# A recurrence with experts behind it: another order for the end of a half, the next preparation, the experts and the skip gate

## The chip, the cores and the metric

The kernel runs on one core of a Trainium2 chip. The metric is device time in microseconds (us) for one execution; the time of a version is the median over its runs. A core has five engines with a queue each: PE (matmul; its weight loads are listed as PEld), DVE (vector), ACT (scalar), POOL (GpSimd) and SP, which here only issues transfers. Each engine takes its instructions in the order of its queue; between engines they wait on semaphores. PE's clock can be granted at less than full speed, and the profile shows the granted share.

## The reference, cut to what matters

Eight layers run one after the other on x of 4 x 1024 tokens with 128 features. The change touches the last two: a selective recurrence with 16 states over 256 channels, and a mixture of eight experts. Each layer adds its result to x and is followed by a layer norm.

```python
# recurrence
x = resid * rsqrt(mean(resid * resid) + EPS) * norm_w
skip = x @ skip_w.T                        # 256 channels
xs = silu(conv4(x @ in_w.T) + conv_b)
delta = softplus(xs @ wd1.T @ wd2.T + wd2_b)
Bm, Cm = xs @ wb.T, xs @ wc.T              # 16 states each
def step(h, inp):                          # along the tokens
    d_l, b_l, c_l, x_l = inp
    h = exp(d_l[:, :, None] * A) * h + (d_l * x_l)[:, :, None] * b_l[:, None, :]
    return (h, einsum('ben,bn->be', h, c_l))
y = (ys + xs * W_D) * silu(skip)
return resid + y @ out_w.T
# experts, all eight computed, gated per token
probs = softmax(x @ Wr + br)
keep = mask of the largest probs up to TOP_P = 0.8
h = relu(einsum('bth,ehf->betf', x, W1) + b1)
y = einsum('betf,efh->beth', h, W2) + b2
return einsum('bte,beth->bth', probs * keep, y)
```

## The kernel before

The last two layers are worked in eight halves: four sequences, two halves of 512 tokens each (`b`, `h`). All is float32. For each half there are four stages, each written as a generator that yields between its steps, so that one loop, `l3`, can interleave them:

- `l3_prepare`: norm and transpose (`sq3`, `xnT`), two products `pxe` with a four-tap convolution on DVE and a silu by tanh (`xs`), the product `pdb`, whose rows for B and C go to memory (`rows`), and then delta: the products `pd0`, `pd1`, a softplus on ACT and DVE (`sp_u`, `sp_w`, through an exponential and a logarithm), and `ud` = delta times `xs` on DVE and `dl` on ACT. It takes ten steps.
- `l3_scan`: sixteen states, one step each. SP loads the state's rows of B and C, broadcast over the partitions (`bn`, `cn`). POOL multiplies `db` = `ud` x `bn` (L1845). ACT makes `da` (L1849), DVE runs the scan along the tokens (L1850, two of them for the 256 channels), POOL multiplies `hc` = `db` x `cn` (L1861). `db` and `hc` have four buffers each. The first half of a sequence hands its last column on as `carry`.
- the states are summed in PSUM by identity products, `pys` (`add`). From the third half on (`b > 0`), `hc` of each odd state is first added to the even one before it by an adding transfer (L1865), and the sum is taken up two states later. `l3_sum` takes up what is left after the last state and adds `xs` times `W_D`.
- `l3_finish`: the skip gate (`psk`, tanh, two DVE operations for each half of the channels), the output product `po`, the residual `ss_r`, the norm, and the router of the experts, which ends in `gt`. The half then goes to the list `todo` with `age` 0.

The experts (`l3_experts`, `l3_ffn_head`, `l3_ffn`) take halves from `todo` once they are older than three states. A head (`pgt`, `gT`, `pb2`) starts the accumulator `h_acc`. Each of the eight experts has four products `ph` with relu on ACT (`hh`), sixteen products `py`, and four operations of DVE into `h_acc` (L1989). Weights (`wh`) are loaded two experts ahead.

In the loop of `l3`, each state of the running half is followed by one step of the end of the half before it (`l3_sum`, then `l3_finish`), one step of the preparation of the next half, one of what is left of the layer before (a mixture with sorted rows: `moe`, its gathers `yg` on POOL and its tiles `wx` on PE), and three or four steps of the experts. What is left of the end and of the preparation after the sixteenth state is written out then.

This order of the text isn't yet the order of the queues: the framework schedules the instructions for each engine when the program is built, and the queue is fixed from then on.

Of the kernel before, what the change touches and what calls it, by code (L numbers as in the profile page):

```python
# [10 lines left out]
F32 = mybir.dt.float32  # L11
I32 = mybir.dt.int32
U32 = mybir.dt.uint32
AF = mybir.ActivationFunctionType
ALU = mybir.AluOpType
# [3 lines left out]
P = 128  # L19
# [21 lines left out]
E3, NST, DDELTA, KCONV = 256, 16, 64, 4  # L41
# [17 lines left out]
class Net:  # L59
# [1535 lines left out]
    def l3(self, moe, fp):  # L1595

        c3 = self.c3  # L1600
        halves = [dict(b=b, h=h) for b in range(B) for h in range(2)]
        for i, u in enumerate(halves):
            u["prev"] = halves[i - 1] if u["h"] else None
        halves[0] = dict(self.c3["first"], **{k: halves[0][k] for k in ("prev",)})
        for i, u in enumerate(halves[1:], 1):
            u["prev"] = halves[i - 1] if u["h"] else None
        work = self.l3_experts(fp)
        end = iter(())
        for i, u in enumerate(halves):
            nxt = iter(())  # L1610
            if i + 1 < len(halves):
                if halves[i + 1]["h"] == 0:
                    while "done" not in self.m2["st"][halves[i + 1]["b"]]:
                        next(moe)
                nxt = self.l3_prepare(halves[i + 1])
            for f in self.l3_scan(u):
                next(end, None)
                next(nxt, None)
                for k in range(1):
                    next(self.m2["rest"], None)  # L1620
                busy = next(moe, moe) is not moe
                if i == 0:
                    for k in range(1):
                        next(moe, None)
                for k in range(3 if busy else 4):
                    next(work)
                for v in c3["todo"]:
                    v["age"] += 1
            for f in chain(end, nxt):
                pass  # L1630
            end = chain(self.l3_sum(u), self.l3_finish(u))
        for f in end:
            next(work)
        c3["all"] = True
        for f in work:
            pass

    def l3_experts(self, fp):


        c3 = self.c3
        heads, self.wh = [], {}

        def others():

            while len(heads) < 2 and c3["todo"] and ("all" in c3 or c3["todo"][0]["age"] > 3):
                heads.append((c3["todo"].pop(0), []))
            return heads[1:]

        i = 0  # L1650
        while True:
            others()
            if "all" in c3 and c3["banks"]:

                c3["banks"].close()
                c3["banks"] = None
                c3["ctx"].enter_context(self.banks(ff=8))
            if heads:
                u = heads[0]
                if not u[1]:  # L1660
                    yield from self.l3_ffn_head(*u, fp)
                yield from self.l3_ffn(*u, i, fp, others)
                heads.pop(0)
                i += NE
            elif "all" in c3:
                return
            else:
                yield
# [146 lines left out]
    def l3_scan(self, u):  # L1815


        nc, c3, b, h = self.nc, self.c3, u["b"], u["h"]
        sp, wp, aneg = c3["sp"], c3["wp"], c3["aneg"]
        wout = c3["we"][:, :, ND:]  # L1820
        xnT, xs, dl, ud, rows = (u[k] for k in ("xnT", "xs", "dl", "ud", "rows"))
        carry = wp.tile([P, 2, NST], F32, name="carry") if h == 0 else u["prev"]["carry"]
        u["carry"] = carry
        u["py"] = py = []
        u["sums"] = sums = []

        def add(n, hc):
            if not py:
                py.extend(self.psb(f"y{ec}", [P, 512], f"pys{ec}") for ec in range(2))
                u["first"] = n  # L1830
            for ec in range(2):
                self.mm(py[ec], self.ident, hc[:, ec, :], n == u["first"], n == NST - 1)

        u["add"] = add
        for n in range(NST):
            bc = []
            for i, nm in enumerate(("bn", "cn")):
                t = wp.tile([P, 1, 512], F32, name=nm, bufs=4)
                r = i * NST + n
                nc.sync.dma_start(  # L1840
                    out=t[:, 0, :], in_=rows[r : r + 1, :].to_broadcast([P, 512])
                )
                bc.append(t.to_broadcast([P, 2, 512]))
            db = wp.tile([P, 2, 512], F32, name="db", bufs=4)
            nc.gpsimd.tensor_mul(db, ud, bc[0])  # L1845
            for ec in range(2):
                j = ec * NST + n
                da = self.psb("da", [P, 512], "da")
                nc.scalar.activation(da, dl[:, ec, :], AF.Exp, scale=aneg[:, j : j + 1])  # L1849
                nc.vector.tensor_tensor_scan(  # L1850
                    db[:, ec, :],
                    da,
                    db[:, ec, :],
                    carry[:, ec, n : n + 1] if h else 0.0,
                    ALU.mult,
                    ALU.add,
                )
            if h == 0:
                nc.scalar.copy(carry[:, :, n : n + 1], db[:, :, 511:512])
            hc = wp.tile([P, 2, 512], F32, name="hc", bufs=4)  # L1860
            nc.gpsimd.tensor_mul(hc, db, bc[1])  # L1861
            if n % 2 and b > 0:

                hc0 = sums.pop()[1]
                nc.gpsimd.dma_start(out=hc0, in_=hc, accum_op=ALU.add)  # L1865
                sums.append((n, hc0, n + 2))
            else:
                sums.append((n, hc, n + 2))
            for k in range(2):
                if sums and sums[0][2] <= n:  # L1870
                    add(*sums.pop(0)[0:2])
            yield

    def l3_sum(self, u):

        while u["sums"]:
            u["add"](*u["sums"].pop(0)[0:2])
            if u["sums"]:
                yield
        for ec in range(2):  # L1880
            x = u["xs"][:, ec, :]
            self.nc.vector.scalar_tensor_tensor(
                x, x, self.col("W_D", i=ec), u["py"][ec], ALU.mult, ALU.add
            )

    def l3_finish(self, u):


        nc, c3, b, h = self.nc, self.c3, u["b"], u["h"]
        sp, wp = c3["sp"], c3["wp"]  # L1890
        ff = lambda s, n: self.psb("ff", s, n)
        wout = c3["we"][:, :, ND:]
        yt = u["xs"]
        for ec in range(2):
            p = ff([P, 512], "psk")
            self.mm(p, c3["wskip"][:, 0, ec * P : (ec + 1) * P], u["xnT"])

            t = sp.tile([P, 512], F32, name="th")
            nc.scalar.activation(t, p, AF.Tanh, scale=0.5)
            nc.vector.scalar_tensor_tensor(p, t, 1.0, p, ALU.add, ALU.mult)  # L1900
            nc.vector.scalar_tensor_tensor(
                yt[:, ec, :], yt[:, ec, :], 0.5, p, ALU.mult, ALU.mult
            )
            yield
        po = ff([P, 4, D], "po")
        for k in range(4):
            for ec in range(2):
                self.mm(
                    po[:, k, :],
                    yt[:, ec, k * P : (k + 1) * P],  # L1910
                    wout[:, ec, :],
                    ec == 0,
                    ec == 1,
                )

        r = sp.tile([P, 4, D], F32, name="ss_r", tag="s2")
        nc.vector.scalar_tensor_tensor(
            r, self.xN[b][:, 4 * h : 4 * h + 4, :], 2.0, po, ALU.mult, ALU.add
        )
        yield  # L1920
        yield from self.norm_parts(wp, r, b, 4 * h, 4, ps=ff, act=True, slow=True)
        yield
        n = NC // 2
        pr, g, rank, pj, cum = self.router(sp, b, c3["wr"], c3["br"], ps=ff, c0=4 * h, n=n)
        q, cum = cum
        nc.vector.tensor_mul(g, q, pj)
        nc.vector.reduce_sum(cum, g, AX.X)

        nc.vector.tensor_single_scalar(cum, cum, TOP_P, ALU.is_lt)
        nc.vector.scalar_tensor_tensor(cum, rank, 1.0, cum, ALU.is_le, ALU.max)  # L1930
        u["gt"] = sp.tile([P, n, NE], F32, name="gt", bufs=8)
        nc.vector.tensor_mul(u["gt"], pr, cum)
        u["age"] = 0
        c3["todo"].append(u)
# [268 lines left out]
```

## Time and profile before

The median of 23 runs is 2343.95 us, from 2334.18 to 2350.4.

| what | value |
|---|---|
| profiled execution | 2342.13 us, of which span 2340.4 us |
| granted clock of PE, mean | 0.92 |
| PE busy | 2007.0 us, 86% |
| DVE busy | 1349.4 us, 58% |
| ACT busy | 1204.8 us, 51% |
| POOL busy | 1024.3 us, 44% |
| `hc` on POOL (L1861) | 128 of 2483 ns |
| `db` on POOL (L1845) | 128; the form of 112 takes 2606 ns |
| scans on DVE (L1850) | 256, of 1207 and 1267 ns |
| `pys` on PE | 320 records, busy 160.5 us |
| adding transfers `hc<-hc` | 48, 512 KB each, 6.6 us to landing |

The profile names an instruction by its line, its engine and the tiles that it writes and reads. A float32 matmul leaves two records. Busy time of PE is a union of overlapping records, since matmuls are pipelined, so that the mean of one times their number is more than the busy time. The layers before the recurrence fill about the first 1400 us of the span; a second stretch, to about 2200 us, holds the eight halves, and the rest the experts of the last two halves. A row of a timeline gives start, length, engine, line, operation, tiles and, in brackets, how long the engine was idle before it and what ended that. A row of windows gives the stretch, its length, then busy time and instruction count of PE, PEld, DVE, ACT and POOL, PE's granted clock, the share of DMA and its GB/s.

### The profile page before, as it was taken

The page shows a single profiled execution, that of the slowest core. Times are in us where ns is not written, and L with a number is a line of the kernel's source. Part 1 is how long each engine was busy: PE and PEld are TensorE (multiplying, and loading weights), DVE is VectorE, ACT ScalarE, POOL GpSimd, SP SyncE. Part 2 cuts the span into 40 slices and gives each one's busy share as a digit, 9 for nine tenths or more (in the row PEclk, how much of TensorE's full clock was granted, in tenths as well). Part 3 has the DMA queues.
Part 4 walks back from the last instruction along what each step waited for, and adds up shares of the span by engine and source line. Part 5 has one row for each costly group of instructions (what it writes and reads, how often), then busy time and mean ns, then how long its engine had stood idle before and what let it go on. Part 6 is the DMA issues. An engine that isn't in the chain of part 4 may idle for free. (4 is left out here: it accounts for less than half of the span.)

```text
span 2340.4 us, 46470 instructions
## 1 busy us (share of the span) xinstructions
PE 2007.0 (86%) x17858; PEld 1408.3 (60%) x17858; DVE 1349.4 (58%) x3661; ACT 1204.8 (51%) x2619; POOL 1024.3 (44%) x813
## 2 busy tenths in 40 slices
PE   6667978979999999999989856778899989799988
PEld 3455654544577777787777654345565556456666
DVE  6458743433445554654555536877777777676421
ACT  6543433332244444454455536566767876657343
POOL 5100220000123244134143239988898988779400
PEclk9657989979999999999999868989999999899899
DMA  3000110013000010031232056556776676666421
GB/s 104 0 17 21 32 36 10 10 65 115 1 3 3 2 37 22 25 87 37 74 87 74 22 171 178 175 164 196 196 204 176 173 196 164 177 177 180 99 59 50
DMA packets 138702, 211.63 MB, mean 90 GB/s; under 512 B 18613, under 2 KB 75952, under 8 KB 138096
## 3 DMA queue, kind: packets, MB, share of 16 engines
q1 hardware_dynamic: 126192, 173.87, 24.6%
q0 software_dynamic: 12288, 34.79, 7.0%
q8 instruction: 141, 2.31, 0.4%
q14 instruction: 81, 0.66, 0.1%
HBM read 160.29 MB, written 23.16 MB: 78 GB/s over the span
## 5 line engine op out<-in xcount | busy, mean ns | idle before, releaser
L1061 POOL TENSOR_TENSOR qt<-r_q,sb_c_turn 128x256 f32<-128x256 f32 (+1 forms) x256 | 163.8, 661 | 453.2 <-ACT r_q L1053 447.6
L1861 POOL TENSOR_TENSOR hc<-db,cn 128x1024 f32<-128x1024 f32 x128 | 314.8, 2483 | 60.0 <-PE pys L127 25.5
L1845 POOL TENSOR_TENSOR db<-ud,bn 128x1024 f32<-128x1024 f32 x112 | 285.9, 2606 | 32.1 <-DVE ud L1809 15.8
L127 PEld LDWEIGHTS py<-wh,hh 128*128 128x128 f32 x2048 | 250.8, 195 | 70.6 <-issue 35.9
L127 PE MATMUL ph<-xT,wh 128*128 128x512 f32 x512 | 261.6, 628 | 24.3 <-ACT hh L1973 9.9
L127 PE MATMUL py<-wh,hh 128*128 128x128 f32 x2048 | 257.2, 280 | 15.9 <-ACT hh L1973 13.8
L1973 ACT ACTIVATE hh<-ph,sb_cols 128x512 f32<-128x512 f32 x256 | 171.4, 681 | 135.2 <-PE ph L127 108.3
L1119 DVE TENSOR_TENSOR a<-pa_m,sb_c_near 128x256 f32<-128x256 f32 x256 | 96.7, 420 | 213.7 <-PE pa_m L127 213.7
L1076 ACT ACTIVATE kN<-kp_mo,sb_c_trig 128x128 f32<-128x128 f32 x448 | 129.7, 371 | 132.4 <-PE kp_mo L131 119.6
L1849 ACT ACTIVATE da<-dl,aneg 128x512 f32<-128x512 f32 x224 | 153.4, 689 | 75.0 <-DVE db L1850 74.1
L127 PE MATMUL pys<-hc,sb_c_ident 128*128 128x512 f32 x320 | 160.5, 627 | 16.0 <-POOL hc L1861 9.2
L1850 DVE TENSOR_TENSOR_SCAN db<-da,carry,db 128x512 f32<-128x512 f32 x128 | 157.2, 1267 | 10.8 <-ACT da L1849 6.2
L127 PEld LDWEIGHTS ph<-xT,wh 128*128 128x128 f32 x512 | 91.3, 199 | 114.5 <-issue 56.0
L1850 DVE TENSOR_TENSOR_SCAN db<-da,db 128x512 f32<-128x512 f32 x128 | 149.8, 1207 | 11.5 <-ACT da L1849 5.7
L1989 DVE SCALAR_TENSOR_TENSOR h_acc<-py,gt,h_acc 128x128 f32<-128x128 f32 x256 | 71.7, 343 | 134.6 <-PE py L127 134.5
L127 PE MATMUL pqk<-xT,wE 128*128 128x256 f32 x512 | 139.2, 396 | 8.0 <-ACT coT L1195 4.3
L127 PEld LDWEIGHTS pys<-hc,sb_c_ident 128*128 128x128 f32 x320 | 60.8, 203 | 78.4 <-issue 57.4
L127 PEld LDWEIGHTS pqk<-xT,wE 128*128 128x128 f32 x512 | 90.7, 198 | 22.3 <-DVE cv L1038 8.1
L1195 ACT COPY coT<-pt 128x512 f32<-128x512 f32 x64 | 37.5, 585 | 127.1 <-PE pt L131 127.1
L729 POOL DMA_INDIRECT orows<-o,ix x20 | 18.9, 944 | 185.8 <-DVE o L727 160.3
L131 PE MATMUL pt<-sb_c_ident,xN 128*128 128x128 f32 x224 | 54.2, 341 | 51.9 <-ACT xN L174 33.4
L127 PE MATMUL po<-ht,wD 128*128 128x512 f32 x192 | 94.1, 598 | 0.0
(450 smaller groups left out, 4370.1 us busy)
## 6 DMA issues: line engine op xcount, KB each, us to landing
wx<-in_wF SPq DMA_DIRECT2D x92, 384.0 KB, 3.3
bn<-rows SPq DMA_DIRECT2D x128, 256.0 KB, 5.1
cn<-rows SPq DMA_DIRECT2D x128, 256.0 KB, 4.5
wh<-in_wH SPq DMA_DIRECT2D x64, 512.0 KB, 3.6
hc<-hc POOLq DMA_DIRECT2D x48, 512.0 KB, 6.6
xrows<-zero SPq DMA_DIRECT2D x4, 1472.0 KB, 9.0
xg<-xrows SPq DMA_DIRECT2D x20, 256.0 KB, 2.9
yrows<-ys SPq DMA_DIRECT2D x20, 256.0 KB, 3.1
```

The lines of the kernel that those rows point to most:

```text
L127: return self.nc.tensor.matmul(out=out, lhsT=lhsT, rhs=rhs, start=start, stop=stop)
L131: self.nc.tensor.transpose(out, in_, self.ident[0:n, 0:n])
L1061: nc.gpsimd.tensor_mul(u["qt"][:, m, a:], u["q"][:, a:], c2["turn"][:, m, o + a : o + 2 * P])
L1076: self.nc.scalar.activation(u["kN"][:, c, m, :], pk[:, c, :], AF.Copy, scale=trig[:, k, m : m + 1])
L1119: nc.vector.tensor_mul(u["a"][:, i, :, :], pa[i], self.c2["near"][:, None, :].to_broadcast([P, 2, P]),)
L1195: nc.scalar.copy(oT, pt)
L1845: nc.gpsimd.tensor_mul(db, ud, bc[0])
L1849: nc.scalar.activation(da, dl[:, ec, :], AF.Exp, scale=aneg[:, j : j + 1])
L1850: nc.vector.tensor_tensor_scan(db[:, ec, :], da, db[:, ec, :], carry[:, ec, n : n + 1] if h else 0.0, ALU.mult, ALU.add,)
L1861: nc.gpsimd.tensor_mul(hc, db, bc[1])
L1973: nc.scalar.activation(ht, ph, AF.Relu, bias=self.col("h_b1", i=e * NK + k))
L1989: nc.vector.scalar_tensor_tensor(acc[:, c, :], py[:, c, :], gt[:, c, e : e + 1], acc[:, c, :], ALU.mult, ALU.add,)
```

## The change

The loop of `l3` takes two steps of the end of the half before per state instead of one. The next half's preparation takes no step in the first four states and one in each of the other twelve. A half is given to the experts from the first state after its router instead of the fourth. The experts get three steps a state in the last half too. The last half's last odd state isn't added by a transfer but summed as it is. The skip gate moves from `l3_finish` to a function of its own, `l3_gate`, which is called in the states 9 and 12 of the half itself and keeps its result in SBUF (`th0`, `th1`, one buffer each) until `l3_sum`; there DVE adds `W_D` times `xs` into the sum in PSUM and multiplies the gate in.

```diff
-            for f in self.l3_scan(u):
-                next(end, None)
-                next(nxt, None)
+            u["final"] = final = i + 1 == len(halves)
+            for n, f in enumerate(self.l3_scan(u)):
+                for k in range(2):
+                    next(end, None)
+                if n > 3:
+                    next(nxt, None)
                 for k in range(1):
                     next(self.m2["rest"], None)
                 busy = next(moe, moe) is not moe
...
-                for k in range(3 if busy else 4):
+                for k in range(3 if busy or final else 4):
                     next(work)
...
-            while len(heads) < 2 and c3["todo"] and ("all" in c3 or c3["todo"][0]["age"] > 3):
+            while len(heads) < 2 and c3["todo"] and ("all" in c3 or c3["todo"][0]["age"] > 0):
                 heads.append((c3["todo"].pop(0), []))
...
             nc.gpsimd.tensor_mul(hc, db, bc[1])
-            if n % 2 and b > 0:
-
+            if n in (9, 12):
+                self.l3_gate(u, n // 12)
+            if n % 2 and b > 0 and not (u["final"] and n == NST - 1):
                 hc0 = sums.pop()[1]
                 nc.gpsimd.dma_start(out=hc0, in_=hc, accum_op=ALU.add)
...
         for ec in range(2):
-            x = u["xs"][:, ec, :]
+            x, p = u["xs"][:, ec, :], u["py"][ec]
             self.nc.vector.scalar_tensor_tensor(
-                x, x, self.col("W_D", i=ec), u["py"][ec], ALU.mult, ALU.add
-            )
+                p, x, self.col("W_D", i=ec), p, ALU.mult, ALU.add
+            )
+            self.nc.vector.scalar_tensor_tensor(
+                x, u["gate"][ec], 0.5, p, ALU.mult, ALU.mult
+            )
+
+    def l3_gate(self, u, ec):
+
+        nc, c3 = self.nc, self.c3
+        p = self.psb("ff", [P, 512], "psk")
+        self.mm(p, c3["wskip"][:, 0, ec * P : (ec + 1) * P], u["xnT"])
+        t = c3["sp"].tile([P, 512], F32, name=f"th{ec}")
+        nc.scalar.activation(t, p, AF.Tanh, scale=0.5)
+        nc.vector.scalar_tensor_tensor(t, t, 1.0, p, ALU.add, ALU.mult)
+        u.setdefault("gate", []).append(t)
...
-        for ec in range(2):
-            p = ff([P, 512], "psk")
-            self.mm(p, c3["wskip"][:, 0, ec * P : (ec + 1) * P], u["xnT"])
-
-            t = sp.tile([P, 512], F32, name="th")
-            nc.scalar.activation(t, p, AF.Tanh, scale=0.5)
-            nc.vector.scalar_tensor_tensor(p, t, 1.0, p, ALU.add, ALU.mult)
-            nc.vector.scalar_tensor_tensor(
-                yt[:, ec, :], yt[:, ec, :], 0.5, p, ALU.mult, ALU.mult
-            )
-            yield
```

## The prediction, before the changed kernel ran

> **What bounds the kernel now.** I read first the busy row of POOL over the span, then the windows cut at the end of each half's last `hc`, then POOL's and PE's timelines at the seam between two halves, then the chain of waits there.
>
> ```profile
> span 2340.4 us, 46470 instructions
> POOL 5100220000123244134143239988898988779400
> 1498.00:1607.00 109.00, 82.23 (x365) 52.98 (x366) 79.01 (x141) 67.81 (x136) 91.93 (x50) 0.89 0.53 160
> 1903.00:1990.00 87.00, 82.80 (x412) 54.54 (x411) 59.92 (x108) 57.35 (x99) 76.05 (x38) 1.00 0.68 177
> 1990.00:2094.00 104.00, 90.63 (x425) 57.70 (x424) 73.97 (x143) 67.98 (x119) 81.60 (x41) 0.92 0.65 175
> 2094.00:2193.00 99.00, 87.74 (x431) 56.96 (x430) 69.45 (x139) 63.65 (x99) 81.23 (x40) 0.93 0.63 173
> 2193.00:2337.00 144.00, 132.10 (x696) 92.69 (x695) 34.24 (x120) 56.03 (x88) 0.88 (x1) 0.94 0.19 54
> ```
>
> POOL is at 8 to 9 tenths from 1400 to 2200 us: that is the recurrence, eight halves of sixteen states (columns of the windows: length, then busy PE, PEld, DVE, ACT, POOL, granted clock). After it PE alone works for 144 us on experts that are left. Half 5 (1903 to 1990) takes 87 us; halves 6 and 7 take 104 and 99 with nearly the same POOL work. The seams say why:
>
> ```profile
> 1982.63 0.87 POOL L1865 DMA_DIRECT2D hc<-hc  x1
> 1988.10 2.34 POOL L1861 TENSOR_TENSOR hc<-db,cn 128x1024 f32<-128x1024 f32 x1 [4.60 <-PE pys L127]
> 2007.42 9.26 POOL L1845 TENSOR_TENSOR db<-ud,bn 128x1024 f32<-128x1024 f32 x4 [15.81 <-DVE ud L1809]
> 2091.55 2.35 POOL L1861 TENSOR_TENSOR hc<-db,cn 128x1024 f32<-128x1024 f32 x1 [5.13 <-PE pys L127]
> 2107.45 9.26 POOL L1845 TENSOR_TENSOR db<-ud,bn 128x1024 f32<-128x1024 f32 x4 [12.37 <-ACT dl L1810]
> ```
>
> POOL stands idle 17.0 us (1990.4 to 2007.4) and 13.5 us (2093.9 to 2107.45) between the last `hc` of a half and the first `db` of the next, which needs `ud`, the end of the preparation. At the earlier seams the next half's `db` starts up to 17 us ahead of the last `hc`, and no seam shows. The chain through the second seam:
>
> ```profile
> 2094.20 7.36 DMA hc<-hc
> 2101.60 1.14 PE pys L127 x2
> 2103.43 0.69 DVE pd L1808
> 2106.03 0.60 DVE ud L1809
> 2106.66 0.58 ACT dl L1810
> ```
>
> The adding transfer lands, PE sums it, DVE passes its wait for that sum, and only then come the last steps of the preparation, queued behind it.
>
> **The change part by part.** The arithmetic keeps its counts: per half two `psk` products, two tanh, six DVE operations, before and after. Removed is one adding transfer of the last half, for which two identity products come (2 x 0.9 us of PE, in a queue that waits there anyway). What changes is order, and this I read from the queues as built for both kernels; they hold no time, so each stretch is counted in matmuls of 512 columns and priced at 0.90 us (four `ph`, x8 in the records, take 3.60).
>
> *Experts earlier.* Behind the last `pys`, PE had 15.75 experts left and has 11.75. Before, from the end of that `pys` (2204.0) to the first `pgt` of the last half (2249.3) went 45.3 us, and from there to the end 91.1 with ten experts. Now nine follow `pgt`: 91.1 - 8.3 = 82.8 (ten took 2249.3 to 2332). To `pgt` goes the chain: two sums and two gate products on DVE 2.9, `po` 1.9, then `ss_r` to `gt` as before (2224.85 to 2241.53, 16.7), and 2 in PE's queue: 23.5. The gate's `psk`, which came 12 us after the last `pys`, no longer stands in it. Tail 106.3 against 136.4: -30.1. From last `hc` to last `pys` went 11.1 with the transfer; without, as at the first seam (1497.9 to 1499.9), 2.0, and I take 2.5: -8.6.
>
> *The preparation later.* It starts four states later, and its `pd` products, which feed the ACT chain to `ud`, move past the half's last `pys`. In PE's queue before, they stood 23 to 62 matmuls ahead of it at five seams and 7 to 9 ahead at the last two. Now they end 19 behind it (seam 1-2), 6.5 (2-3), 17 (4-5), 6.5 (5-6) and 6.5 (6-7); only 0-1 (9 ahead) and 3-4 (23 ahead) stay open. PE takes its queue in order, so at five seams the whole chain now runs after the half's end. Its price:
>
> ```profile
> 2091.30 1.88 PE L127 MATMUL pd<-db,sb_s_d 65*128 65x512 f32 x4
> 2092.36 0.60 ACT L1795 ACTIVATE sp_u<-pd 128x512 f32<-128x512 f32 x1 [1.66 <-PE pd L127]
> 2098.73 1.06 ACT L1802 ACTIVATE sp_w<-sp_w 128x1024 f32<-128x1024 f32 x1
> 2101.60 1.98 PE L127 MATMUL pys<-hc,sb_c_ident 128*128 128x512 f32 x4 [2.69 <-DMA hc<-hc]
> ```
>
> Last `hc` to the end of `pys` takes 13.4, 9.7 and 11.1 at the three ends that have a transfer last, 11.4 in the mean; 2.0 without. Then PE's stretch to `pd`: 6.5 x 0.90 = 5.9, or 15.3 and 17.1. From `pd`'s end (2093.18) to the logarithm's (2099.79) 6.6, at the seam before 7.5: 7.05. Then two sums and two products on DVE, 2.7. Four `hh` of 0.69 now stand inside ACT's chain: 0 to 2.8, I take 1.4. So a seam costs 28.4 (2-3, 5-6, 6-7), 37.8 (4-5) and 30.2 (1-2, no transfer; eight gathers of 1.26 fill 10 of it). At 0-1 it is 3: nine matmuls ahead is 8 us, the chain 11. Behind these waits on DVE stand the experts' `h_acc`; PE has three to four and a half experts (24 to 37 us) queued ahead of the next `pys`, so it has work for most of a seam. SP's loads of the next `bn` and `cn` (5.1 and 4.5 us) wait for `rows`, written before `pd`; they land inside the seam, and without that cover would cost about 6.
>
> *Bodies.* First `db` to last `hc` took 86.5 and 85.5 in halves 6 and 7: 86 with transfers; half 0, 98.8 with sixteen gathers at 1.26, is 78.6 without. Half 1: 3 + 78.6 = 81.6. Half 2: 30.2 + 86 + 10.1 (eight more gathers) = 126.3; PE's queue has 134 matmuls there, at 0.94 us (the 785 of the whole rest were busy 740 us) also 126. Half 3: 28.4 + 86 + 20.2 (sixteen gathers) + 2.3 (one `db` of half 4) = 136.9. Half 4, no seam: 84. Half 5: 123.8. Half 6: 114.4. Half 7: 113.4 with one transfer less. Sum 780.4 against 695.0 (1497.9 to 2192.9): +85.4.
>
> **Sum:** +85.4 - 8.6 - 30.1 = +46.7 on the profiled run's 2342.1 (its span 2340.4 and 1.7 around it): 2388.8. The median of the runs is 1.8 above that run: 2390.
>
> Granted clock: half 5 without a seam had 1.00, halves 6 and 7 with one 0.92 and 0.93. [...]
>
> **Rivals.**
> (1) The seams stay as they were and the experts' gain is paid out: -8.6 - 30.1 gives 2305. For it: the end's two steps a state free `xs` and the shared tiles earlier, and before, five of seven seams cost nothing. Against: `pd` stands behind the last `pys`. It decides if POOL's added idle stays under 39 us, under half of what I count.
> (2) PE is the true bound and the seams only move its idle about. For it: PE is busy 82.8 of 87 us in half 5, and experts now lie ready to fill a seam. PE's rest after the first half is 792 matmuls against 785, with 100 us of idle unchanged: +7, 2351. Against: halves 6 and 7 show 13 and 11 us of PE idle with experts queued.
> (3) The crowded halves 2 and 3 (134 and 122 matmuls) bind PE and POOL by turns, PE's in-order waits for `hc` holding experts back: half 2 runs at the 92% of half 3 (104.3 of 113), half 3 too loses 8, and ACT's `hh` cost their full 2.8: +26, 2416.
>
> **How the numbers follow.** My forecast 0.66, with its own range 2361 to 2424 (low: transfer 9.7, no `hh`, bodies 2 shorter; high: 13.4, 2.8, bodies 2 longer, half 2 at 92%). Rival 1 0.10, rival 2 0.12, rival 3 0.12, mostly inside that range. The range goes down to 2346 to take in rival 2. A measurement here tells about 0.2% (4.7 us) from no change: faster 0.10, within 0.05 (the low part of rival 2), slower 0.85.
>
> **What would show it.** Right: in POOL's timeline five idle stretches of 25 to 40 us ended by `ud` or `dl` ahead of four `db` in a row (10 us of gathers inside the first); `pd` after the last `pys` at these seams; last `pys` near 2286 and some 106 us behind it. Wrong: the seams under 15 us each, or `pd` on PE before the last `pys`; a tail still of 130 us; or half 2 and 3 stretched with POOL waiting for `pys` instead of `ud`.

## The result, and the profile after

The changed kernel takes 2414.91 us (median of 8 runs, 2404.71 to 2418.93) against 2342.78 us of the kernel before beside it (62 runs): ratio 1.0305, 95% interval 1.0288 to 1.0321, so slower by 72 us. Lines of the page of its profiled execution, with the row of `db` on POOL:

```profile
span 2411.9 us, 46476 instructions
PE 2033.9 (84%) x17862; PEld 1419.6 (59%) x17862; DVE 1358.0 (56%) x3661; ACT 1204.6 (50%) x2617; POOL 1022.4 (42%) x812
...
POOL 5001310000232252242243188948488939494900
...
L1848 POOL TENSOR_TENSOR db<-ud,bn 128x1024 f32<-128x1024 f32 x112 | 284.1, 2650 | 130.5 <-DVE ud L1812 71.8
```

The same row of the kernel before:

```profile
L1845 POOL TENSOR_TENSOR db<-ud,bn 128x1024 f32<-128x1024 f32 x112 | 285.9, 2606 | 32.1 <-DVE ud L1809 15.8
```

POOL's row over the span, at 7 to 9 through the recurrence before, now falls to 3 or 4 in five slices, one at each seam that opens. `db` waits 130.5 us in all where it waited 32.1. The windows cut at the last `hc` of a half (length, busy PE, PEld, DVE, ACT, POOL, granted clock) come next: the seven halves behind the first, then the tail (from the last `hc` of all to the end), then half 2:

```profile
1501.00:2295.00 794.00, 670.97 (x3145) 434.34 (x3146) 527.78 (x996) 492.00 (x895) 591.07 (x303) 0.92 0.59 161
2295.00:2411.90 116.90, 98.21 (x530) 69.15 (x528) 27.66 (x101) 41.88 (x68) 0.04 (x1) 0.93 0.16 49
1577.50:1723.70 146.20, 124.90 (x659) 87.40 (x659) 94.90 (x203) 98.01 (x203) 95.77 (x55) 0.95 0.65 179
```

The first two of these windows in the kernel before:

```profile
1497.90:2192.90 695.00, 606.89 (x2935) 395.20 (x2936) 510.83 (x971) 476.35 (x870) 592.26 (x303) 0.95 0.65 180
2192.90:2340.40 147.50, 132.20 (x697) 92.78 (x695) 34.24 (x120) 56.03 (x88) 0.91 (x2) 0.93 0.19 54
```

The recurrence is 99 us longer, the tail 30.6 shorter, half 0 ends 3.1 later: 71.5 in all. POOL's work in it is the same (591 and 592 us). PE is busy 30 us longer over both windows together (769.2 against 739.1), with 43 records more in them (3675 against 3632, most of them left over from the layer before), and idle 38 us longer (141.7 against 103.4). POOL's timeline at the seams 1-2, 4-5 and 6-7 (in brackets the idle time before):

```profile
1619.03 9.29 POOL L1848 TENSOR_TENSOR db<-ud,bn 128x1024 f32<-128x1024 f32 x4 [18.62 <-DVE ud L1812]
...
1946.99 2.34 POOL L1864 TENSOR_TENSOR hc<-db,cn 128x1024 f32<-128x1024 f32 x1 [1.93 <-PE pys L127]
1983.18 9.31 POOL L1848 TENSOR_TENSOR db<-ud,bn 128x1024 f32<-128x1024 f32 x4 [32.68 <-ACT dl L1813]
...
2181.82 2.35 POOL L1864 TENSOR_TENSOR hc<-db,cn 128x1024 f32<-128x1024 f32 x1 [4.24 <-PE pys L127]
2211.30 9.29 POOL L1848 TENSOR_TENSOR db<-ud,bn 128x1024 f32<-128x1024 f32 x4 [25.94 <-ACT dl L1813]
```

From the last `hc` of a half to the first `db` of the next, the seams are now 0, 41.6 (with eight gathers in it), 28.9, -4.7, 33.9, 26.6 and 27.1 us; before they were 0, -17.1, -8.8, -10.6, -10.2, 17.0 and 13.5. The chain of waits through the last of them:

```profile
2192.57 1.72 PE pys L127 x4
...
2199.13 0.88 PE pd L127 x2
...
2208.68 1.29 DVE pd L1811 x2
2209.97 0.60 DVE ud L1812
2210.60 0.58 ACT dl L1813
```

`pd` stands behind `pys` on PE, and `dl` ends 11 us after `pd`: the chain that the prediction drew.

PE itself is not held up by the seams. Windows of the seam 4-5 and of the rest of half 5 behind it:

```profile
1949.30:1983.20 33.90, 31.39 (x152) 19.76 (x151) 17.58 (x35) 22.40 (x41) 0.92 (x3) 1.00 0.47 127
1983.20:2072.00 88.80, 71.95 (x322) 45.41 (x321) 62.94 (x112) 48.81 (x81) 80.20 (x39) 0.87 0.58 151
```

In the seam PE is idle 2.5 us at the full clock; in the 88.8 us behind it, 16.9 us with a clock of 0.87. The other seams that open are alike: in all five together, 158 us, PE is idle 14 us and never at half clock. Of its 138 us of idle time up to the last instruction 109 lie in the seven bodies (first `db` to last `hc`; before, 77 of 100), and of its 142 us at half clock 130.

### The profile page after: what moved, and what is told of

It is laid out like the page before. It is cut to its first block, busy times and chain, and to the rows that moved or that the text cites. A ratio compares the mean times of both kernels' runs of the same rounds, so it can differ in the third digit from the quotient of the medians.

```text
span 2411.9 us, 46476 instructions
## 1 busy us (share of the span) xinstructions
PE 2033.9 (84%) x17862; PEld 1419.6 (59%) x17862; DVE 1358.0 (56%) x3661; ACT 1204.6 (50%) x2617; POOL 1022.4 (42%) x812
## 4 chain that ended last, share of the span: by engine, by line
PE 43%; DVE 13%; ACT 8%; issue 3%; DMA 3%; POOL 2%; SPq 0%; ACTq 0%; POOLq 0%; DVEq 0%
PE ph L127 7%; PE py L127 6%; DVE db L1853 5%; PE po L1128 5%; PE pqk L127 4%; PE pa_m L127 4%; PE pys L127 3%; PE kp_mo L127 3%; PE pr_sx L1198 2%; PE pv L127 2%; PE pt L131 1%; DMA hc<-hc 1%; ACT hh L1979 1%; POOL db L1848 1%; PE kp_mo L131 1%
## 5 line engine op out<-in xcount | busy, mean ns | idle before, releaser
L1848 POOL TENSOR_TENSOR db<-ud,bn 128x1024 f32<-128x1024 f32 x112 | 284.1, 2650 | 130.5 <-DVE ud L1812 71.8
L127 PE MATMUL pys<-hc,sb_c_ident 128*128 128x512 f32 x324 | 176.9, 677 | 45.9 <-DMA hc<-hc 25.6
```

The costliest lines, as they stand in the source:

```text
L127: return self.nc.tensor.matmul(out=out, lhsT=lhsT, rhs=rhs, start=start, stop=stop)
```

## The experiments

The changed kernel has four parts that can be undone or made alone: the late start of the preparation, two steps of the end per state, experts at age over 0, and the gate in its own half. The table gives for each run its ratio to the kernel before in the same job (runs made together on one chip), and from its trace the sum of the seven seams, the sum of the seven bodies, the time from the last `hc` of all to the last instruction, and PE's busy and idle time from the end of half 0 to there (us; the last instruction ends some 3.4 us before the span).

| run | ratio | seams | bodies | last `hc` to end | PE busy | PE idle |
|---|---|---|---|---|---|---|
| before | 1 | -16 | 711 | 144 | 739 | 100 |
| after | 1.0305 | 153 | 641 | 113 | 769 | 138 |
| e1 after, preparation from the first state | 1.0275 | 118 | 653 | 130 | 764 | 137 |
| e2 after, gate in the end | 1.0411 | 129 | 691 | 116 | 768 | 167 |
| e3 before, preparation late | 1.0049 | 59 | 658 | 141 | 748 | 110 |
| e4 after, no addition at any end | 1.0306 | 154 | 641 | 113 | 772 | 136 |
| e5 after, age over 3 | 1.0080 | 90 | 652 | 113 | 753 | 101 |
| e6 after, end one step | 1.0179 | 102 | 662 | 113 | 748 | 129 |
| e7 before, age over 0 | 1.0041 | 17 | 674 | 157 | 741 | 107 |
| e8 before, end two steps | 1.0072 | 74 | 650 | 132 | 752 | 104 |
| e9 after, age over 3, end one step | 1.0004 | 63 | 660 | 124 | 744 | 104 |
| e10 before, gate moved | 0.9896 | 6 | 691 | 132 | 741 | 87 |
| e11 before, last half's gate only | 0.9996 | -18 | 722 | 140 | 740 | 104 |
| e12 after, preparation first, two steps | 1.0182 | 71 | 672 | 150 | 773 | 120 |

**e1.** The late start alone is undone.

```diff
-                if n > 3:
-                    next(nxt, None)
+                next(nxt, None)
```

> The changed kernel with one line undone: the preparation takes a step in every state again, from the first. Theory (the place of pd in PE's queue sets the seam): pd now ends 18 matmuls ahead of the half's last pys at seam 0-1, 11.5 and 11 ahead at 1-2 and 4-5, 20 ahead at 3-4, 1 ahead at 6-7, and 3 and 8 behind at 2-3 and 5-6. So POOL's idle at 1-2 falls from 41.6 us to under 10, at 4-5 from 33.9 to about 15, at 2-3, 5-6 and 6-7 it stays at 20 to 30; the tail has two experts more (13.8 against 11.75, +16 us). About 45 us less than the changed kernel: 2370, from 2355 to 2385. Rival (the gate or the double steps of the end cost the time, the preparation's start does not): within 10 us of 2415. Rival (all of the loss is the late start): 2343 - 38 = 2305.

Measured 2407.57 us, ratio 1.0275 (1.0229 to 1.0322): a miss. The seams shrank by 35 us, but the bodies took 12 of it and the tail 17, with 14.3 experts left for it in place of 12 (counted in records of `py`). So the late start, undone in the changed kernel, gives back 7 us of the 72, less than the interval of this ratio can tell from nothing.

**e2.** The gate goes back into the end; the late start, the two steps and the age stay.

```diff
-            if n in (9, 12):
-                self.l3_gate(u, n // 12)
...
     def l3_finish(self, u):
...
+        for ec in range(2):
+            self.l3_gate(u, ec)
+            self.nc.vector.scalar_tensor_tensor(
+                yt[:, ec, :], u["gate"][ec], 0.5, yt[:, ec, :], ALU.mult, ALU.mult
+            )
+            yield
```

> The changed kernel with the skip gate back in l3_finish, all else as changed. Theory (place of pd): without psk in the states the schedule puts pd 10.5 behind the last pys at 1-2 instead of 18, and 1 to 5 ahead at 2-3, 4-5, 5-6 and 6-7 instead of behind; seams of about 30, 23, 18, 20 and 22 us instead of 41.6, 28.9, 33.9, 26.6 and 27.1, some 45 less, and psk back in the chain of the tail, +5: 2375, from 2360 to 2392. Rival (the gate's work is hidden and its place is nothing): 2415 plus 5 for the tail, 2420.

Measured 2437.83, ratio 1.0411 (1.0368 to 1.0455): a miss in sign. The five open seams came within 5 us each of the expected ones (126 in all against 113); the bodies grew by 50, which I had not counted. PE's timeline shows one of the places:

```profile
1895.62 0.77 PE L127 MATMUL po<-sb_s_e,xs 128*128 128x128 f32 x2 [15.81 <-DVE xs L1908]
```

`po` stands in PE's queue and waits for the gate's multiplication (`xs`, L1908); PE idles 15.8 us there. That this is where the 50 us come from is read from this place and not tested. With the other three parts in place, moving the gate gains: 1.0411 - 1.0305 is 25 us of 2343.

**e3.** The kernel before with the late start alone.

```diff
-            for f in self.l3_scan(u):
+            for n, f in enumerate(self.l3_scan(u)):
                 next(end, None)
-                next(nxt, None)
+                if n > 3:
+                    next(nxt, None)
```

> The kernel before with one thing of the change: the preparation takes no step in the first four states. Theory (place of pd, not the number of states): pd stays ahead of the last pys at every seam, by 12, 50, 11, 30, 9, 6 and 6 matmuls, so no seam has the full 28 us; 2-3 and 4-5 open to some 15 us because ud stands behind DVE's wait for pys, and the last two stay near 17 and 13.5. About +32 in seams and -8 in the tail (14.7 experts left behind the last pys against 15.75): 2367, from 2350 to 2385. Rival (four states' delay by itself makes the loss of the change): seams of 28 us at five places, 2425 or more. Rival (the delay is hidden): 2343 less 8.

Measured 2356.32, ratio 1.0049 (1.0029 to 1.0068), within the range. The seams rise by 75 us and the time by 12: the bodies fall by 53 (711 before, 658 here), so most of what a seam adds comes off POOL's waits inside the bodies.

**e4.** No last state is added by a transfer, in any half.

```diff
-            if n % 2 and b > 0 and not (u["final"] and n == NST - 1):
+            if n % 2 and b > 0 and n < NST - 1:
```

> The changed kernel, where the last odd state of every half, not of the last half alone, is summed as it is instead of being added by a transfer. The queues stay nearly as they are (pd 18, 4, 13.75, 7 and 5.5 behind the last pys). Theory (a seam is a sum of terms, of which the way from the last hc to the last pys is one): that way was 13.3, 8.8, 9.6 and 10.1 us at the seams 2-3, 4-5, 5-6 and 6-7 and 7.7 at the end of the last half, where no transfer ends it, so each of the four seams gives back 2 to 5 us: 2400, from 2392 to 2408. Rival (the transfer's latency is the seam, the preparation only fills it): 9 us or more from each of the four, 2376 or less.

Measured 2415.25, ratio 1.0306 (1.0264 to 1.0347): no change where 2392 to 2408 was expected, a miss, and the seams stay at 154. From the last `hc` to the end of the last `pys` the seams 2-3, 4-5, 5-6 and 6-7 took 16.3, 9.1, 9.6 and 12.6 us without a transfer, and 13.3, 8.7, 9.7 and 10.1 with it. So the transfer, which the prediction charged with 11.4 of the 28.4 us of a seam, is not what sets it. Each state summed by itself costs PE two products more, some 1.8 us (an estimate: four `ph` took 3.60), which may hide a small gain.

**e5.** The age alone is undone.

```diff
-            while len(heads) < 2 and c3["todo"] and ("all" in c3 or c3["todo"][0]["age"] > 0):
+            while len(heads) < 2 and c3["todo"] and ("all" in c3 or c3["todo"][0]["age"] > 3):
```

> The changed kernel with the experts begun only at an age over 3, as before; all else as changed. In the built queue of PE the first pd of the next half then stands, against the last pys of the half, at -12, +6, -24, -3, -20 and -10 (in matmuls of 512 columns) for the seams 1-2 to 6-7, where the changed kernel has +17, +4, -24, +14, +1 and +1. By the runs so far a seam costs about 24 us plus 1 us for each such matmul, so the seams come to some 11, 29, -2, 21, 3 and 14 us, 76 in place of 153. Theory (the three parts of the schedule work together: what is put between pys and pd on PE makes the seam, and a body gives a part of it back, since POOL has its waits there instead): a third to a half of the 77 us is given back, so 2360 to 2390 us, about 2376. Rival (experts begun at once cost nothing, since their matmuls only fill PE's idle time): 2405 to 2420, no change. Second rival (nothing is given back in the bodies): 2338.

Measured 2360.38, ratio 1.0080 (1.0054 to 1.0106), at the low edge of the theory's range: 53 of the 72 us go with this line, and the tail keeps its gain (113 us). PE's queue at the end of half 1 shows why that seam goes (41.6 to 7.3 us). First the changed kernel, then e5:

```profile
1578.32 1.02 PE L127 MATMUL ph<-xT,wh 128*128 128x512 f32 x2
1579.18 1.02 PE L127 MATMUL psk<-xnT,sb_s_in 128*128 128x512 f32 x2
1580.04 1.02 PE L127 MATMUL pxe<-xnT,sb_s_in 128*128 128x512 f32 x2
1580.89 3.60 PE L127 MATMUL pys<-hc,sb_c_ident 128*128 128x512 f32 x8
...
1586.53 3.60 PE L127 MATMUL pys<-hc,sb_c_ident 128*128 128x512 f32 x8
...
1607.13 1.88 PE L127 MATMUL pd<-db,sb_s_d 65*128 65x512 f32 x4
```

```profile
1581.45 1.88 PE L127 MATMUL pd<-db,sb_s_d 65*128 65x512 f32 x4
...
1592.33 1.88 PE L127 MATMUL pys<-hc,sb_c_ident 128*128 128x512 f32 x4
```

In the first, `pd` starts 17 us after the end of the last `pys`; in the second, 11 us before the last `pys` starts. The second thing that goes is idle time of PE, 138 to 101 us. PE's waits from 1498 to 2310 us (engine, what waits, what it waits for: total us, times, longest), in the changed kernel and in e5:

```profile
PE pys L127 <- DMA hc<-hc: 25.6, 9, 8.1
PE pgt L131 <- DVE gt L1938: 20.6, 5, 5.8
...
PE pt L131 <- ACT xN L174: 11.1, 2, 5.5
```

```profile
PE pys L127 <- DMA hc<-hc: 20.5, 7, 4.5
...
PE pgt L131 <- DVE gt L1938: 7.9, 3, 6.1
```

`pgt`, the head of a half's experts, needs `gt`, the last step of its router. In the kernel before PE waited for it 4.1 us, once. The same work in both kernels, behind half 5: the norm's transposes `pt`, the router's product `prl`, and in the changed kernel, which comes first, `pgt`:

```profile
2111.64 3.74 PE L127 MATMUL py<-wh,hh 128*128 128x128 f32 x32
2120.91 1.63 PE L131 MATMUL pt<-sb_c_ident,xN 128*128 128x128 f32 x4 [5.53 <-ACT xN L174]
2125.61 3.78 PE L127 MATMUL pys<-hc,sb_c_ident 128*128 128x512 f32 x4 [3.08 <-DMA hc<-hc]
2129.19 1.40 PE L127 MATMUL prl<-sb_h_router,xT 128*128 128x8 f32 x8
...
2138.86 1.02 PE L131 MATMUL pgt<-sb_c_ident,gt 128*8 128x128 f32 x4 [5.78 <-DVE gt L1938]
```

```profile
2072.95 0.60 PE L131 MATMUL pt<-sb_c_ident,xN 128*128 128x128 f32 x4
2073.39 0.39 PE L127 MATMUL py<-wh,hh 128*128 128x128 f32 x2
2073.61 1.02 PE L127 MATMUL ph<-xT,wh 128*128 128x512 f32 x2
2074.47 3.06 PE L127 MATMUL py<-wh,hh 128*128 128x128 f32 x26
...
2084.19 3.82 PE L127 MATMUL py<-wh,hh 128*128 128x128 f32 x32
```

With experts begun at once, no product of theirs stands between `pt` and `pgt` here, and PE runs dry through the router's chain: it is busy 19.1 us of the 34.7 from 2107.8 to 2142.5. At an age over 3, products of experts (`ph`, `py`) lie in between (`pgt` comes at 2100.1), and PE is busy 24.2 us of 33.8 (2072.0 to 2105.8). This is one place, with 15.6 us of idle time against 9.6; over the whole stretch the waits for `gt` fall by 13 us of the 37 that PE idles less, so the rest lies in other waits.

**e6.** The end's pace alone is undone.

```diff
-                for k in range(2):
-                    next(end, None)
+                next(end, None)
```

> The changed kernel with the end of a half at one step a state, as before; all else as changed. The first pd stands at -18, +12, -24, +2, -9 and -12 against the last pys at the seams 1-2 to 6-7; by 24 us plus 1 us for each, seams of 5, 34, -2, 26, 15 and 12 us, 90 in place of 153, and 0.8 of an expert more is left for the tail (some 7 us). Theory: with a third to a half of the 63 us given back in the bodies, 2375 to 2400, about 2384. Rival (the end's two steps are what puts its chain ahead of pys, so it alone made the loss): 2335 to 2360. Rival (it plays no part): 2405 to 2420.

Measured 2383.73, ratio 1.0179 (1.0154 to 1.0205), as the theory had it: 30 us. PE's idle time (129) and its waits for `gt` (19.2 us) change little, while its busy time falls from 769 to 748. So 30 us can go with the waits for `gt` still there.

**e7, e8.** The kernel before with the age alone (the edit of e5 reversed), and with two steps of the end alone.

> The kernel before with one part of the change alone: experts begin at an age over 0. In PE's built queue the first pd stands at -57, -34, -32, -17, 0 and -7 against the last pys (before: -62, -44, -50, -35, -8, -8), still ahead of it at all seams but 5-6; as many experts are left for the tail as before (15.9). Seams by the same rule some 25 us in all against -16 before. Theory (no part alone makes the loss, since the body gives back most of a seam while pd stands ahead of pys): 2348 to 2366, about 2355. Rival (experts at once are the cause): 2375 to 2400.

> The kernel before with one part of the change alone: a half's end at two steps a state. The first pd stands at -50, -30, -14, -3, -3 and -7 against the last pys; one expert less is left for the tail (14.7 against 15.75, some -9 us). Seams some 52 us in all against -16. Theory (no part alone makes the loss): most of it is given back in the bodies as in the run with the late preparation alone, 2336 to 2362, about 2348. Rival (the end's two steps are the cause): 2375 to 2400.

Measured 2350.22 (1.0041, 1.0024 to 1.0057) and 2358.37 (1.0072, 1.0054 to 1.0089), both in the theory's ranges, e8 at the top of its own. In e7 PE waits 27.9 us for `gt`, more than in the changed kernel, and the whole is 10 us slower: the wait alone does not make the loss either.

**e9.** The edits of e5 and e6 together.

> The changed kernel with two parts undone, the experts' age over 3 and a half's end at one step a state; left of the change are the preparation from the fifth state, the gate in its own half and the last half's missing addition. The first pd stands at -36, -5, -24, -1, -17 and -13 against the last pys at the seams 1-2 to 6-7; by the rule, seams of 0, -6, 19, 0, 23, 7 and 11 us, 54 in all (153 after), bodies of some 655, and 13 experts left for the tail (11.75 after, some 9 us). Theory: end of the first half 1499 + 54 + 655 + 121 from the last hc + 4 around the span = 2333, with the other runs' spread 2325 to 2352. Rival (the two parts undone overlap fully, so that nothing comes on top of the age alone): 2352 to 2366.

Measured 2382.15, ratio 1.0004 (0.9987 to 1.0021) to the kernel before, which took 2382.78 in this job (see the last section); scaled to 2342.8 that is 2344 us (2340 to 2348), inside the theory's spread and below the rival's. Without these two parts the loss is gone. With them it stays when either other part is undone (e1 1.0275, e2 1.0411). The two alone on the kernel before were not run.

**e10, e11.** The kernel before with the gate moved, the last half's three steps and missing addition, and the preparation's step ahead of the end's (its diff, in part); and the kernel before with only the last half's gate moved and its last addition left out.

```diff
             for n, f in enumerate(self.l3_scan(u)):
+                for k in range(1):
+                    next(nxt, None)
                 next(end, None)
-                next(nxt, None)
...
+            if n in (9, 12):
+                self.l3_gate(u, n // 12)
```

> The kernel before with the gate in its own half, the last half's fourth step and missing addition, and the preparation's step ahead of the end's; its start, the end's pace and the experts' age are as before. The first pd stands at -54, -42, -44, -34, -8 and -20 against the last pys, as before within 8 matmuls but at 6-7. Theory (the gate's move is the part that gains, some 22 us in the changed kernel, but here the bodies have less to give, since the end's chain was not behind a seam): seams of some 0 in all, bodies 700, from the last hc to the end 132, sum 1499 + 0 + 700 + 132 + 4 = 2335, range 2322 to 2345, so 0 to 18 faster than before. Rival (the gate gains only where the seam is long): 2340 to 2350.

> The kernel before, changed in its last half alone: its gate is worked out in states 9 and 12, and its last state is not added to the one before it. Everything up to the last hc is as before. Theory: from the last hc to the last pys 7.7 us as in the changed kernel, in place of 11.1, and 3 matmuls of 512 columns fewer behind it (some 3 us): 2330 to 2338, about 2335. Rival (the experts behind the last pys fill PE whatever the chain does): 2338 to 2344.

e10 is the version that beats both: 2358.05 us, ratio 0.9896 (0.9870 to 0.9921), 25 us below the kernel before, more than the 0 to 18 expected (scaled, 2318 us against a range from 2322). The gate's move was not run here without the preparation's place ahead of the end, which may have a share. e11 is no gain, 2381.4 us, 0.9996 (0.9980 to 1.0012), as its rival said. Windows of e10, recurrence and tail:

```profile
1528.90:2225.70 696.80, 618.31 (x2983) 399.21 (x2982) 514.62 (x977) 484.34 (x883) 593.17 (x304) 0.96 0.67 181
2225.70:2360.90 135.20, 122.84 (x682) 87.54 (x680) 32.85 (x118) 51.30 (x83) 0.02 (x1) 0.97 0.19 55
```

Against e11 of the same job the seven halves take 7 us less and the rest 8 less, with twelve records of PE fewer (682 against 694) and a granted clock of 0.97 against 0.94. From the end of half 0 on, PE has its least idle time of all runs, 87 us, and its least time at half clock, 67 us.

**e12.** The changed kernel with the preparation first, two steps a state, from the first state on; experts at once, two steps of the end and the moved gate stay.

```diff
-                for k in range(2):
-                    next(end, None)
-                if n > 3:
-                    next(nxt, None)
+                for k in range(2):
+                    next(nxt, None)
+                for k in range(2):
+                    next(end, None)
```

> The changed kernel, but the next preparation goes two steps a state from the first state on and ahead of the end's two steps; experts begin at once, the end goes two steps and the gate stands in its own half as changed. The first pd stands at -46, -54, -32, -7, -11, +1 and 0 against the last pys (after: -10, +17, +4, -24, +14, +1, +1), and 15.9 experts are left for the tail (11.75 after, some 40 us). Theory (what makes the loss is the place of pd behind pys, not the experts as such): seams of 0, -9, -2, 15, 12, 25 and 24 us, 65 in all, bodies of some 655, 1499 + 65 + 655 + 141 from the last hc + 4 = 2364 on a chip where the kernel before takes 2342, so a ratio near 1.009 (1.000 to 1.016). Rival (experts begun at once and two end steps crowd PE whatever the preparation's place, as in the changed kernel with the preparation from the first state alone): ratio 1.02 to 1.03.

Measured 2418.34 against 2376.43 in its job, ratio 1.0182 (1.0160 to 1.0204): above my range and just below the rival's. The seams came to 71 us against the expected 65, the bodies to 672 against 655, the time from the last `hc` to 150 against 141. So the place of `pd` tells the seams well enough, but it doesn't explain the loss: with half of the seams gone, 43 of the 72 us stay, some of them because 16 experts are left for the tail as in the kernel before.

## Why the prediction was right, and where it was not

The range and the sign were met, and the seams opened where and by the chain that was said. But the loss isn't the price of these seams, as e1, e3 and e12 show, so that the time lies in the range is in part luck. Term by term:

**The tail** (-30.1): 109.2 us from the last `pys` (2302.7) to the end in place of 106.3. The size is right, the reason isn't: it was priced as the gain of the experts' earlier start, but undoing that start keeps it (e5, 12 experts left for the tail and 113 us), and that start alone leaves 16 experts, as before, and a tail of 157 us (e7). No part made alone leaves clearly fewer (e3 and e8 also 16); which of them together do it, the runs don't isolate.

**Last `hc` to last `pys`** (2.5): measured 7.7. No transfer is in it, as said; but three products of `ph` and then `pys` of three states, not of one, stood in PE's queue behind that `hc`: 2.2 us for the rest of `ph`, 5.5 for the sums. The step that took 2.0 from the first seam was mis-sized.

**The seams** (156 in all as worked out): 153 measured. The position of `pd` in the queue was read rightly, and the sum hits; its parts do less so. Seam 1-2 was put at 30.2 and took 41.6. The same 2.0 was at fault: it took 12.6 from the last `hc` to the end of `pys`, since four states' sums and 5.6 us of other products were still ahead, as the first fence under e5 shows. At the seams with a transfer the 11.4 charged to it was PE's queue instead: without any transfer (e4) the seams stay. That 11.4 was also the mean of the last three of six ends with a transfer; at the other three this stretch took 19.0, 18.7 and 17.7 us in the kernel before. What was read rightly is that PE has work for most of a seam: it idles 14 us in 158.

**The bodies** (the forecast's 780.4 less its seams: 624): 641 measured. Half 2, at 86 + 10.1, took 104.7, with 12.1 us of POOL waiting for `pys`, the longest 7.6; half 4, at 84, took 91.9.

**The sum** (+46.7): +71.5. The recurrence makes 13.6 of the difference, last `hc` to `pys` 5.2, the end of half 0 3.1, the tail 2.9. The sign and the chain were right; the largest term mis-sized is half 2, 146.3 against 126.3.

**What the sum could not show.** It counted POOL's time, where a seam adds what it adds. The experiments show that it isn't so: 75 us of seams cost 12 in e3, and 35 us less gained 7 in e1. The trace shows the loss on PE too, as 38 us of idle time and 30 us more of busy time. What makes it is the age with the end's two steps (e9); made alone on the kernel before they cost 10 and 17 us (e7, e8), undone alone in the changed one they give 53 and 30. On PE the age undone takes off 37 us of idle and 16 of busy time, the two steps undone 9 and 21. Adding the four parts, each made alone on the kernel before (for the gate, e10 with the small edits that came with it), gives 12 + 10 + 17 - 25 = 14 us; the changed kernel loses 72. The prediction priced the late preparation as the whole cause and the age as the tail's gain; the age's other side, longer waits and a lower clock of PE in the bodies, was in none of its steps. How much of it comes from the waits for `gt`, from the experts that PE has worked off in the seams and from the clock, the runs don't part.

**The rivals.** The first (seams unchanged, 2305) fell with the seams. The second (2351, PE's idle time unchanged at 100) fell in the changed kernel with 138; e5, without the age, comes close to its numbers: 101 us of idle and 2360. The third (2416) met the time, not the halves: half 2 at 92% would be 137 and half 3 145; they took 146 and 138.

**The clock.** The prediction put the granted clock of halves 6 and 7, 0.92 and 0.93, beside their seams and gave it no term in its sum. The trace has no half clock in the seams: at the five open ones the clock is full, and 130 of the 142 us at half clock lie in the bodies. From the end of half 0 to the last instruction the clock records give 93 us at half clock before, 142 after, 101 in e5, 107 in e6, 67 in e10 and 149 in e12. PE was busy in 71 us of the 93 and in 111 of the 142. In the changed kernel four records of `pys` took 3.78 us at half clock (2125.61) and 1.88 at the full one (2148.59), twice the time, so half of the difference of 40, 20 us by this estimate, is most of PE's 30 us of added busy time. In e5 PE is busy 83 us at half clock and in e6 72, so that by the same estimate 14 and 19 us of their gains go the same way.

Whether the clock costs time by itself or only with the idle time that comes with it, no run tells apart. That stays open.

## What to carry to other kernels

A stage that starts as soon as its input can be had isn't free on an engine that, like PE here, works off its queue in order: its first instruction can put that engine to wait for the chain that feeds it, with no older work left to fill the wait, as behind half 5 here, where PE stood idle 5.8 us before `pgt`. Before pricing a new order from one engine's gaps, close the ledger on the other engine that works most, busy and idle time alike, since a gap on the first can take the place of waits that it had anyway (75 us of seams cost 12 in e3). Try the parts of a reordering one by one: here one part of four gains 25 us, and two others together lose 70 beside it, though each of them made alone costs no more than 17.

## What the runs showed of the hardware

The clock records of the kernel before (76) and of the changed one (96) show PE's clock either full or at half, in stretches that are multiples of 3.41 us but for the last record of each (6.16 and 7.44 us). Around a stretch of the changed kernel in which PE was idle for 8.1 us (windows as above):

```profile
2002.20:2010.30 8.10, 0.00 (x1) 0.00 (x1) 6.23 (x19) 4.11 (x8) 8.10 (x6) 0.81 0.84 226
2010.30:2017.50 7.20, 4.62 (x11) 2.21 (x12) 4.39 (x5) 6.36 (x12) 7.20 (x5) 0.74 0.88 214
2017.50:2034.50 17.00, 13.78 (x30) 6.93 (x30) 12.64 (x25) 5.94 (x11) 16.43 (x9) 0.50 0.61 152
```

The records have half clock from 2007.2 us for 6.8 us, full clock for 3.4, then half for 17.1, in which PE was busy 13.78 us. Why the clock fell, and why it stayed down so long, no run shows.

The kernel before took 2340 to 2345 us in two jobs and 2376 to 2383 in two others, so times are compared by ratio within a job. e11 is the kernel before up to its last half, and its half 0 ends 32.5 us later. Of PE's waits before that point in e11:

```profile
PE ph L127 <- issue: 16.7, 3, 8.9
PE pav L127 <- issue: 8.5, 2, 8.3
```

In the kernel before, such waits, for nothing that the profile shows ("issue"), come to 5.2 us up to the end of half 0; in e11 to 35.9, while its other waits are shorter. In all PE is 16.8 us longer idle there and 15.7 us longer busy for the same 14228 records, at a granted clock of 0.89 against 0.91. What holds the instructions up, the trace does not tell.
